# A tile per half for layer 0's state, sums moved within steps, and outer products spread over other steps, in a two-layer recurrent kernel

## The chip, the cores and the metric

The kernel runs on one core of a Trainium2 chip. The metric is device time in microseconds (us) for one execution. The kernel before takes 1827.79 us (median of 3 runs, 1827.32 to 1827.85). Beside the timed runs there is one profiled execution, and every duration quoted below is from it.

## What is computed

Two recurrent layers over 128 sequences of 128 steps with 512 features, each with a residual, all in float32:

```python
def layer0(x, h, W, b, alpha):          # W is 512 x 1024
    Wh, Wz, leak = W[:, :512], W[:, 512:], 1.0 - alpha
    def step(h, z_t):
        gate = sigmoid(h @ Wh.T + z_t @ Wz.T + b)
        h = tanh(h * leak + gate * z_t)
        return h, h
    ...
def layer1(x, h, Wx, Wh, b):
    xw = x @ Wx + b                      # for all steps
    def step(h, xw_t):
        h = tanh(xw_t + h @ Wh)
        return h, h
    ...
x = x + layer0(x, cond, ...)
x = x + layer1(x, cond, ...)
```

The products with `Wh` have to go step by step. The products of the inputs (`z_t @ Wz.T` and `x @ Wx`) do not depend on the recurrence.

## The kernel before

**Layout.** Features lie on the 128 partitions: a state of one step is a tile of 128 partitions by 4 blocks of 128 features by 128 sequences (`[P, C, P]`, C = 4). "Half 0" of a state is feature blocks 0 and 1, "half 1" blocks 2 and 3. Weights are the stationary operand.

**Steps and groups.** Time runs over steps t = 0 to 136. Layer 0 works on its time t in step t, layer 1 on its time u = t - 9 (`LAG`). Four steps make a group (`G = 4`); k is the place of a step in its group, g the group's number. A step's work on TensorE is, in this order: layer 0's state product (`L0.state_product`, both halves, 3.57 us), layer 1's state product (3.57 us), and some of the *outer products* that prepare the inputs of a later group.

**Input products by Strassen's scheme.** The input product of a whole group is done with seven products in place of eight, numbered 1 to 7 and run in the order `OUTER = 1, 5, 6, 3, 7, 2, 4`. For layer 1 this is one level (`Layer.multiply`: eight matmul instructions of 256 columns, 1.73 us). For layer 0 it is two levels (`DeepLayer.multiply_deep`: each outer product is again seven inner products, in the order `INNER = 1, 2, 6, 3, 7, 4, 5`, 1.56 us), but for its group 1, which is one level, and its group 0, whose inputs are multiplied directly in steps (`input_product`).

The products need sums of activations. Sums of the outer level are made by GpSimd (`add_up`, tiles `sa` for layer 0 and `sb` for layer 1; numbers 5, 6, 3 and 7). Sums of the inner level for layer 0 are made by VectorE (`add_up_inner`, tile `inner`): with `kind` 0 from the activations themselves, called *raw* here, with `kind` 1 from GpSimd's outer sums, called *nested*. A nested sum reads all four of GpSimd's sums. Outer product 1 reads raw sums, outer product 5 nested ones.

Results of products go through PSUM banks A0, A1, B0 and B1. For layer 1, products 1, 6, 7 and 4 share bank B0, products 5 and 3 share B1, product 2 has A1. After each product its bank is read: products 1, 5 and 6 are copied by ScalarE into kept tiles, 3, 7 and 2 are added to a kept tile by VectorE (`add`, L283; `add_deep`, L418), and 4 is copied out last. Product 4 adds onto what stands in the bank of product 7, so it may start only when the add of product 7 has read that bank. For layer 0's deep products, `gather` (VectorE) then combines the parts.

**A step of layer 0.** Before its state product, the bank of the step is filled with the input part: `seed_deep` on VectorE (on ScalarE for group 1). The bank tile `ra` spans two PSUM banks, one per half; it has one buffer, so `bank_of(t + 1)` waits until step t's bank has been read. The state product adds onto it. Then for each half i: `gate0` (ScalarE, two sigmoids), `mix0` (VectorE, one multiplication and two multiply-adds), `tanh0` (ScalarE), and `residual` (GpSimd, adds the state to the activation in place). The next step's state product needs both halves of the new state.

**A step of layer 1.** It has a tile for each half, `r0b` and `r1b`: `seed` (ScalarE) fills it, the state product adds onto it, `tanh1` reads it, `residual` adds it to the activation, and `finish` transposes the result on VectorE to `o` (L168) and stores it.

**Inputs.** `load_x` brings the input of step t + 8 by DMA from SyncE, `prepare_x` transposes it on VectorE (L163) into the group's tile `T`.

**Order of the work.** Each engine works its instructions strictly in the order given. That order is written out by hand: `at(time, fn, ...)` puts a piece of work into a plan with a due time, and at the end the pieces are issued in the order of their due times. A due time sets the order and nothing else; an engine starts an instruction as soon as those before it are done and its inputs are there. `start[t]` is the planned start of step t, worked out from the planned durations (`STATE`, `PRODUCT`, `DEEP`) and from `shares(t)`, which says for each step which outer products of which layer and group it does:

- k = 0: layer 1, group g - 2, products 7, 2, 4
- k = 1: layer 0, group g + 1, products 1, 5, 6, 3
- k = 2: layer 0, group g + 1, products 7, 2, 4
- k = 3: layer 1, group g - 1, products 1, 5, 6, 3

Before step 0, group 1's products 1, 5, 6, 3 and 7 of layer 0 are done; products 2 and 4 follow in steps 3 and 4. In the step with k = 0 that starts at `a` (the next one starting at `b`), GpSimd's sums for group g + 1 are due at a+0.8, 0.9, 4.8 and 8.4; VectorE's raw sums 5, 6, 3 and 7 at a+6.0, 6.7, 7.4 and 9.6, its nested ones at a+11.4, a+12.0, b+5.9 and b+6.6. Layer 0's mix of half 0 is due at a+2.29, of half 1 at a+4.07, the seed of the next step at a+5.31, the adds of layer 1's products 7 and 2 at a+8.92 and a+10.65.

Of the kernel before, what the change touches and what calls it, by code (L numbers as in the profile page):

```python
# [7 lines left out]
F32 = mybir.dt.float32  # L8
AF = mybir.ActivationFunctionType
ALU = mybir.AluOpType  # L10
# [3 lines left out]
def kernel(  # L14
# [56 lines left out]
    psum = ctx.enter_context(tc.tile_pool(name="psum", bufs=1, space=bass.MemoryType.PSUM))  # L71
# [3 lines left out]
    def at(time, fn, *args):  # L75
        plan.append((time, len(plan), fn, args))


    STATE, PRODUCT, DEEP = 3.57, 1.73, 1.56
    OUTER = 1, 5, 6, 3, 7, 2, 4  # L80

    def shares(t):

        g, k = divmod(t, G)
        if t < 5:
            return {3: [(0, 1, OUTER[5:6])], 4: [(0, 1, OUTER[6:])]}.get(t, [])
        said = (
            [(1, g - 2, OUTER[4:])], [(0, g + 1, OUTER[:4])],
            [(0, g + 1, OUTER[4:])], [(1, g - 1, OUTER[:4])],
        )[k]  # L90
        return [x for x in said if 0 <= x[1] < NG]

    start, clock = [], 24.3
# [44 lines left out]
    per_feature = const.tile([P, 3, C], F32, tag="per_feature", name="per_feature")  # L138
# [77 lines left out]
    class Layer:  # L216
# [104 lines left out]
        def state_product(self, t, half, h):  # L321
            alone = (t, half) not in self.state
            ps = self.state_bank(t, half) if alone else self.state[t, half]
            for m in range(2):
                for c in range(C):
                    nc.tensor.matmul(  # L326
                        ps[:, m], self.wh[:, c, 2 * half + m, :], h[t - 1][:, c],
                        start=alone and m == 0 and c == 0, stop=c == C - 1, skip_group_check=True,
                    )
# [3 lines left out]
    class DeepLayer(Layer):  # L333
# [118 lines left out]
            eng.tensor_tensor(c[:, :, 2:4], c[:, :, 2:4], c[:, :, 0:7:6], ALU.add)  # L452
            eng.tensor_tensor(c[:, :, 4], c[:, :, 4], c[:, :, 2], ALU.add)

        def bank_of(self, t):
            self.state[t] = psum.tile([P, 2, 4, P], F32, tag="ra", name=f"ra_{t}")
            return self.state[t][:, :, 0:2]

        def seed_deep(self, t):
            g, k = divmod(t, G)  # L460
            c = self.parts[g, k // H]
            out = self.bank_of(t)
            if g == 1:
                nc.scalar.copy(out, c[:, :, k % H : 4 : H])  # L464
            elif k % H == 0:
                nc.vector.tensor_tensor(out, c[:, :, 0:3:2], c[:, :, 1:4:2], ALU.add)  # L466
            else:
                u3 = c[:, :, 4:5].broadcast_to([P, 2, 2, P])
                nc.vector.tensor_tensor(out, c[:, :, 5:7], u3, ALU.add)  # L469

        def state_product(self, t, half, h):
            for m in range(2):
                for c in range(C):
                    nc.tensor.matmul(  # L474
                        self.state[t][:, half, m], self.wh[:, c, 2 * half + m, :], h[t - 1][:, c],
                        start=False, stop=c == C - 1, skip_group_check=True,
                    )

        def input_product(self, t):

            g, k = divmod(t, G)
            ps = self.bank_of(t)
            for c in range(C):
                for m in range(C):
                    nc.tensor.matmul(
                        ps[:, m // 2, m % 2], self.w[:, c, m, :], ring[g][:, c, k],
                        start=c == 0 and m % 2 == 0, stop=False, skip_group_check=True,
                    )

    L0, L1 = DeepLayer("a"), Layer("b")  # L490
    ring = {}
    h0, h1, s0 = {-1: condT}, {-1: condT}, {}
# [14 lines left out]
    def gate0(t, i):  # L507
        if i == 0:
            s0[t] = work.tile([P, C, P], F32, tag="s", name=f"s_{t}")
            h0[t] = hpool.tile([P, C, P], F32, tag="h0", name=f"h0_{t}")  # L510
        for m in range(2):
            f = 2 * i + m
            nc.scalar.activation(  # L513
                s0[t][:, f], L0.state[t][:, i, m], AF.Sigmoid, bias=per_feature[:, 0, f : f + 1]
            )

    def mix0(t, i):
# [48 lines left out]
    for i, time in ((5, 16.2), (6, 17.4), (3, 18.7), (7, 20.0)):  # L566
        at(time, L0.add_up, 1, i)
    L0.products(1, OUTER[:1], 14.4)
    L0.products(1, OUTER[1:5], 17.4)
    at(18.2, from_natural, condT, cond_in)  # L570
    for kc in range(C):
        at(18.9 + 0.6 * kc, transpose_w0, L0.wh, "wh0", kc)
# [15 lines left out]
    for t in range(T + LAG):  # L588
        g, k = divmod(t, G)
        now = start[t]  # L590
        if AHEAD <= t + AHEAD < T:
            at(now + 0.01, load_x, t + AHEAD)
        if t < T:
            for i in range(2):
                end = now + STATE * (1 + i) / 2
                at(now + STATE * i / 2, L0.state_product, t, i, h0)
                at(end + 0.05, gate0, t, i)
                at(end + 0.5, mix0, t, i)
                at(end + 1.75, tanh0, t, i)
                at(end + 2.3, residual, t, i, h0)  # L600
            if G <= t + 1 < T:
                at(start[G] - 0.9 if t == G - 1 else end + 1.74, L0.seed_deep, t + 1)
            now += STATE
        if t < G - 1:
            at(now + 0.6, L0.input_product, t + 1)
            now += STATE
        u = t - LAG
        if u >= 0:
            for i in range(2):
                end = now + STATE * (1 + i) / 2  # L610
                at(now + STATE * i / 2, L1.state_product, u, i, h1)
                at(end + 0.05, tanh1, u, i)
                if u + 1 < T:
                    at(end + 0.5 if (u + 1) % G else now + STATE + 2 * PRODUCT + 0.1, L1.seed, u + 1, i)
                at(end + 0.6, residual, u, i, h1)
            at(start[t + 1] + 0.6 if u + 1 < T else end + 1.4, finish, u)
            now += STATE
        for layer, group, which in shares(t):
            if layer == 1:
                now = L1.products(group, which, now)  # L620
            elif group == 1:
                now = L0.products(group, which, now)
            else:
# [56 lines left out]
```

## Time and profile before

| what | us |
|---|---|
| median of 3 runs | 1827.79 |
| profiled execution, its own time | 1823.2 |
| its span, first to last instruction | 1821.4 |
| TensorE busy in it | 1694.3 (93%), 13108 matmul instructions |
| VectorE busy | 1047.6 (58%), 1804 instructions |
| ScalarE busy | 657.4 (36%), 1792 instructions |
| GpSimd busy | 806.9 (44%), 788 instructions |
| mean granted TensorE clock | 0.990 |

In the names of the profile PE is TensorE, PEld its weight loads, DVE VectorE, ACT ScalarE, POOL GpSimd and SP SyncE; L474 is line 474 of the kernel. A line of a group or a timeline names the engine, the line, the operation, and output <- input. `ra` is layer 0's state bank, `B_b` one of the product banks B0 and B1 used by layer 1. A float32 matmul of 128 by 128 stands in it as two instructions, so that a state product has 32.

Some step starts of the profiled execution, read from the first matmul of layer 0's state product (layer 1's in step 128):

| step | starts at (us) |
|---|---|
| 0 | 28.3 |
| 3 | 59.0 |
| 4 | 68.8 |
| 6 | 97.2 |
| 8 | 120.8 |
| 12 | 176.55 |
| 40 | 564.2 |
| 41 | 579.1 |
| 42 | 593.2 |
| 43 | 605.0 |
| 44 | 619.1 |
| 124 | 1721.4 |
| 128 | 1764.8 |
| end of the span | 1821.4 |

The four steps from 564.2 are a group in the middle of the run, and those on either side of it look the same. VectorE is busy there for 10.6, 8.6, 8.0 and 6.2 us of the four steps, GpSimd for 10.0, 7.4, 4.1 and 3.5 us, and the 16 DMA engines for about a fifth of the time.

### The profile page before, as it was taken

The page shows a single profiled execution, that of the slowest core. Times are in us where ns is not written, and L with a number is a line of the kernel's source. Part 1 is how long each engine was busy: PE and PEld are TensorE (multiplying, and loading weights), DVE is VectorE, ACT ScalarE, POOL GpSimd, SP SyncE. Part 2 cuts the span into 40 slices and gives each one's busy share as a digit, 9 for nine tenths or more (in the row PEclk, how much of TensorE's full clock was granted, in tenths as well). Part 3 has the DMA queues.
Part 4 walks back from the last instruction along what each step waited for, and adds up shares of the span by engine and source line. Part 5 has one row for each costly group of instructions (what it writes and reads, how often), then busy time and mean ns, then how long its engine had stood idle before and what let it go on. Part 6 is the DMA issues. An engine that isn't in the chain of part 4 may idle for free.

```text
span 1821.4 us, 33397 instructions
## 1 busy us (share of the span) xinstructions
PE 1694.3 (93%) x13108; PEld 1623.3 (89%) x13108; DVE 1047.6 (58%) x1804; ACT 657.4 (36%) x1792; POOL 806.9 (44%) x788
## 2 busy tenths in 40 slices
PE   5789999999999999999999999999999999999998
PEld 5679988899988998988999989899889999889988
DVE  4455666655656656656556656556666556566431
ACT  1233333333333344333333333333333333333433
POOL 3443454443445444444434444434544444454343
PEclk9899999999999999999999999999999999999999
DMA  8101111111211121111121111111111112111112
GB/s 168 36 7 31 40 36 36 42 41 36 45 38 36 36 47 36 40 43 36 36 47 36 36 41 42 36 44 39 36 35 42 41 36 47 36 36 24 25 29 48
DMA packets 153213, 73.78 MB, mean 41 GB/s; under 512 B 16800, under 2 KB 151968, under 8 KB 153056
## 3 DMA queue, kind: packets, MB, share of 16 engines
q1 hardware_dynamic: 148992, 69.53, 17.2%
q10 hardware_dynamic: 3840, 1.84, 0.5%
q8 instruction: 104, 1.70, 0.4%
q14 instruction: 53, 0.43, 0.1%
q0 software_dynamic: 224, 0.27, 0.1%
HBM read 38.02 MB, written 33.55 MB: 39 GB/s over the span
## 4 chain that ended last, share of the span: by engine, by line
PE 71%; DVE 21%; ACT 6%; issue 1%; DMA 1%; POOL 0%; ACTq 0%; POOLq 0%; DVEq 0%
PE ra L474 25%; PE B_b L257 16%; PE A_a L392 8%; DVE inner L199 7%; PE r0b L326 7%; PE r1b L326 7%; PE B_a L392 7%; DVE s L521 6%; ACT s L513 4%; DVE s L519 4%; ACT h L526 2%; DVE cb L283 1%; DVE ra L469 1%; DVE ra L466 1%; DMA x<-in_x_dram 1%
## 5 line engine op out<-in xcount | busy, mean ns | idle before, releaser
L530 POOL TENSOR_TENSOR T<-T,h 128x256 f32<-128x256 f32 x512 | 454.9, 902 | 838.3 <-ACT h L526 800.7
L474 PE MATMUL ra<-h,wha 128*128 128x128 f32 x4064 | 486.0, 279 | 11.1 <-ACT ra L464 6.4
L474 PEld LDWEIGHTS ra<-h,wha 128*128 128x128 f32 x4064 | 480.3, 196 | 16.1 <-ACT ra L464 7.2
L519 DVE TENSOR_TENSOR s<-s,T 128x256 f32<-128x256 f32 x256 | 133.5, 522 | 419.1 <-ACT s L513 419.1
L513 ACT ACTIVATE s<-ra,per_feature 128x128 f32<-128x128 f32 x512 | 158.3, 360 | 492.1 <-PE ra L474 484.8
L326 PE MATMUL r0b<-h,whb 128*128 128x128 f32 x2032 | 249.0, 275 | 0.1
L326 PE MATMUL r1b<-h,whb 128*128 128x128 f32 x2032 | 247.7, 275 | 0.0
L326 PEld LDWEIGHTS r0b<-h,whb 128*128 128x128 f32 x2032 | 237.8, 192 | 1.3 <-ACT h L541 1.1
L326 PEld LDWEIGHTS r1b<-h,whb 128*128 128x128 f32 x2032 | 237.1, 192 | 0.0
L526 ACT ACTIVATE h<-s 128x256 f32<-128x256 f32 x256 | 106.7, 417 | 352.4 <-DVE s L521 352.4
L521 DVE SCALAR_TENSOR_TENSOR s<-h,leak,s 128x128 f32<-128x128 f32 x508 | 184.0, 403 | 9.0
L257 PE MATMUL B_b<-sb,wcb 128*128 128x256 f32 x768 | 176.5, 379 | 1.9 <-ACT kb_p L266 1.9
L199 POOL TENSOR_TENSOR sa<-T 128x512 f32<-128x512 f32 x62 | 94.4, 1522 | 167.5 <-DVE T L163 167.5
L257 PEld LDWEIGHTS B_b<-sb,wcb 128*128 128x128 f32 x768 | 141.3, 190 | 22.5 <-issue 2.3
L392 PE MATMUL A_a<-inner,wia 128*128 128x128 f32 x720 | 139.9, 276 | 0.0
L257 PE MATMUL B_b<-T,wcb 128*128 128x256 f32 x256 | 66.5, 404 | 68.9 <-DVE cb L283 68.9
L257 PEld LDWEIGHTS B_b<-T,wcb 128*128 128x128 f32 x256 | 47.4, 194 | 86.0 <-DVE cb L283 80.5
L392 PE MATMUL B_a<-inner,wia 128*128 128x128 f32 x540 | 107.6, 281 | 11.2 <-DVE inner L199 11.1
L392 PEld LDWEIGHTS A_a<-inner,wia 128*128 128x128 f32 x720 | 110.0, 193 | 0.0
L283 DVE TENSOR_TENSOR cb<-B_b,kb_u 128x512 f32<-128x512 f32 x32 | 22.1, 692 | 149.5 <-PE B_b L257 149.5
L168 DVE STREAM_TRANSPOSE o<-T 128x512 f32<-128x512 f32 x128 | 90.0, 703 | 28.4 <-POOL T L530 25.2
L418 DVE TENSOR_TENSOR ca<-B_a,ka_u 128x512 f32<-128x512 f32 (+1 forms) x60 | 36.9, 625 | 107.6 <-PE B_a L392 107.6
(124 smaller groups left out, 2339.7 us busy)
## 6 DMA issues: line engine op xcount, KB each, us to landing
out_dram<-o SPq DMA_DIRECT2D x510, 64.0 KB, 1.8
x<-in_x_dram SPq DMA_DIRECT2D x502, 64.0 KB, 2.5
wx_in<-in_L_cond_Wx_dram SPq DMA_DIRECT2D x4, 256.0 KB, 5.8
wh_in<-in_L_cond_Wh_dram SPq DMA_DIRECT2D x4, 256.0 KB, 7.5
x<-in_x_dram ACTq DMA_DIRECT2D x10, 64.0 KB, 3.9
wz_in<-in_L_cond_W_dram ACTq DMA_DIRECT2D x2, 256.0 KB, 6.5
wz_in<-in_L_cond_W_dram SPq DMA_DIRECT2D x2, 256.0 KB, 6.0
wh_in<-in_L_cond_W_dram ACTq DMA_DIRECT2D x2, 256.0 KB, 6.4
```

Source lines behind the costliest of these rows:

```text
L168: nc.vector.transpose(dst.rearrange("p a (c j) -> p c a j", j=S), src.rearrange("p c (a i) -> p c a i", i=S))
L199: eng.tensor_tensor(out(SUM[which]), one(), two(), op)
L257: nc.tensor.matmul(ps[:, m], w[:, c, m, :], a[:, c], start=first and m == 0 and c == 0, stop=c == 1, skip_group_check=True,)
L283: nc.vector.tensor_tensor(self.result(g, i, half), banks[tag], self.kept[kept], ALU.add)
L326: nc.tensor.matmul(ps[:, m], self.wh[:, c, 2 * half + m, :], h[t - 1][:, c], start=alone and m == 0 and c == 0, stop=c == C - 1, skip_grou ...
L392: nc.tensor.matmul(banks[f"{tag}{part}"][:, place], self.right_inner(outer, i), self.left_inner(g, outer, i), start=first and place == 0, ...
L474: nc.tensor.matmul(self.state[t][:, half, m], self.wh[:, c, 2 * half + m, :], h[t - 1][:, c], start=False, stop=c == C - 1, skip_group_che ...
L513: nc.scalar.activation(s0[t][:, f], L0.state[t][:, i, m], AF.Sigmoid, bias=per_feature[:, 0, f : f + 1])
L519: nc.vector.tensor_tensor(s[:, two[i]], s[:, two[i]], at_of(t)[:, two[i]], ALU.mult)
L521: nc.vector.scalar_tensor_tensor(s[:, m], h0[t - 1][:, m], leak[:, m : m + 1], s[:, m], ALU.mult, ALU.add)
L526: nc.scalar.activation(h0[t][:, two[i]], s0[t][:, two[i]], AF.Tanh)
L530: nc.gpsimd.tensor_tensor(r, r, h[t][:, two[i]], ALU.add)
```

## The change

The state bank of layer 0 loses its own tile over two banks; layer 0 now uses the same `state_bank` and `state_product` as layer 1, with tiles `r0a` and `r1a`, one per half. `seed_deep` takes a half and makes one instruction per half, due behind the mix of its half. `gate0` takes its half's tile.

```diff
-        def bank_of(self, t):
-            self.state[t] = psum.tile([P, 2, 4, P], F32, tag="ra", name=f"ra_{t}")
-            return self.state[t][:, :, 0:2]
-
-        def seed_deep(self, t):
+        def seed_deep(self, t, half):
             g, k = divmod(t, G)
-            c = self.parts[g, k // H]
-            out = self.bank_of(t)
+            c = self.parts[g, k // H][:, half]
+            out = self.state_bank(t, half)
             if g == 1:
-                nc.scalar.copy(out, c[:, :, k % H : 4 : H])
+                nc.scalar.copy(out, c[:, k % H : 4 : H])
             elif k % H == 0:
-                nc.vector.tensor_tensor(out, c[:, :, 0:3:2], c[:, :, 1:4:2], ALU.add)
+                nc.vector.tensor_tensor(out, c[:, 0:3:2], c[:, 1:4:2], ALU.add)
             else:
-                u3 = c[:, :, 4:5].broadcast_to([P, 2, 2, P])
-                nc.vector.tensor_tensor(out, c[:, :, 5:7], u3, ALU.add)
-
-        def state_product(self, t, half, h):
...
+                nc.vector.tensor_tensor(out, c[:, 5:7], c[:, 4:5].broadcast_to([P, 2, P]), ALU.add)
...
-            ps = self.bank_of(t)
+            ps = [self.state_bank(t, half) for half in range(2)]
...
-                        ps[:, m // 2, m % 2], self.w[:, c, m, :], ring[g][:, c, k],
+                        ps[m // 2][:, m % 2], self.w[:, c, m, :], ring[g][:, c, k],
...
+        ps = L0.state.pop((t, i))
         for m in range(2):
             f = 2 * i + m
             nc.scalar.activation(
-                s0[t][:, f], L0.state[t][:, i, m], AF.Sigmoid, bias=per_feature[:, 0, f : f + 1]
+                s0[t][:, f], ps[:, m], AF.Sigmoid, bias=per_feature[:, 0, f : f + 1]
             )
...
-            if G <= t + 1 < T:
-                at(start[G] - 0.9 if t == G - 1 else end + 1.74, L0.seed_deep, t + 1)
+                if G <= t + 1 < T:
+                    at(end + 1.66, L0.seed_deep, t + 1, i)
```

The sums of activations get other due times within the step with k = 0 and the one behind it, with their own times for the first such step (t = 4), where they are due in step 3 and at the start of step 4:

```diff
-            a, b, f = start[t], start[t + 1], 0.5 if t == G else 1.0
+            a, b = start[t], start[t + 1]
             if g + 1 < NG:
-                for i, time in ((5, 0.8), (6, 0.9), (3, 4.8), (7, 8.4)):
-                    at(a + f * time, L0.add_up, g + 1, i)
-                for i, time in ((5, 6.0), (6, 6.7), (3, 7.4), (7, 9.6)):
-                    at(a + f * time, L0.add_up_inner, g + 1, 0, i, nc.vector)
-                for i, time in ((5, a + 11.4 * f), (6, a + 12.0 * f), (3, b + 5.9 * f), (7, b + 6.6 * f)):
-                    at(time, L0.add_up_inner, g + 1, 1, i, nc.vector)
+                for i, pool, raw, nested in (
+                    (5, a + 1.5, a + 1.45, b + 1.45), (6, a + 7.0, a + 5.8, b + 5.8),
+                    (3, a + 9.0, a + 6.5, b + 6.5), (7, a + 10.0, a + 7.2, b + 7.2),
+                ):
+                    if t == G:
+                        n = (5, 6, 3, 7).index(i)
+                        pool, raw, nested = start[3] + 2.5 + n, start[3] + 5.8 + 0.1 * n, a + 0.2 + 0.1 * n
+                    at(pool, L0.add_up, g + 1, i)
+                    at(raw, L0.add_up_inner, g + 1, 0, i, nc.vector)
+                    at(nested, L0.add_up_inner, g + 1, 1, i, nc.vector)
...
-            at((start[2] + 1.1, start[3] + 0.5, start[3] + 1.2, start[3] + 4.5)[t], prepare_x, t + AHEAD)
+            at((start[2] + 1.1, start[2] + 6.0, start[3] + 0.3, start[3] + 1.0)[t], prepare_x, t + AHEAD)
```

The outermost products of the first and last groups go to other steps. At the start: group 1's product 2 before step 0 (its product 4 in step 3), group 2's products 1 and 5 in step 4, 6 and 3 in step 5. At the end: group 30's products of layer 1 in steps 125 to 127, group 31's in steps 128 to 132, where they stood in 127 and 128, and in 131 and 132. The planned start of step 0 goes from 24.3 to 26.0, and the seed of layer 1 at a group's border may be due earlier:

```diff
-        if t < 5:
-            return {3: [(0, 1, OUTER[5:6])], 4: [(0, 1, OUTER[6:])]}.get(t, [])
-        said = (
-            [(1, g - 2, OUTER[4:])], [(0, g + 1, OUTER[:4])],
-            [(0, g + 1, OUTER[4:])], [(1, g - 1, OUTER[:4])],
-        )[k]
+        if t <= G + 1:
+            return {
+                3: [(0, 1, OUTER[6:])], 4: [(0, 2, OUTER[:2])], 5: [(0, 2, OUTER[2:4])]
+            }.get(t, [])
+        if g == NG - 1:
+            said = (
+                [(1, g - 2, OUTER[4:])], [(1, g - 1, OUTER[:2])],
+                [(1, g - 1, OUTER[2:4])], [(1, g - 1, OUTER[4:])],
+            )[k]
+        elif t >= T:
+            said = [(1, NG - 1, (OUTER[0:1], OUTER[1:2], OUTER[2:3], OUTER[3:5], OUTER[5:])[t - T])] if t < T + 5 else []
+        else:
+            said = (
+                [(1, g - 2, OUTER[4:])], [(0, g + 1, OUTER[:4])],
+                [(0, g + 1, OUTER[4:])], [(1, g - 1, OUTER[:4])],
+            )[k]
...
-    L0.products(1, OUTER[1:5], 17.4)
+    L0.products(1, OUTER[1:6], 17.4)
...
-                    at(end + 0.5 if (u + 1) % G else now + STATE + 2 * PRODUCT + 0.1, L1.seed, u + 1, i)
+                    due = min(now + STATE + 2 * PRODUCT + 0.1, start[t + 1] - 0.05)
+                    at(end + 0.5 if (u + 1) % G else due, L1.seed, u + 1, i)
```

More of the change, by code (lines that the diff above doesn't have):

```diff
@@ L84, in shares @@
         g, k = divmod(t, G)
-        if t < 5:
-            return {3: [(0, 1, OUTER[5:6])], 4: [(0, 1, OUTER[6:])]}.get(t, [])
-        said = (
-            [(1, g - 2, OUTER[4:])], [(0, g + 1, OUTER[:4])],
-            [(0, g + 1, OUTER[4:])], [(1, g - 1, OUTER[:4])],
-        )[k]
+        if t <= G + 1:
[14 more added lines that the diff above has]
+            )[k]
         return [x for x in said if 0 <= x[1] < NG]
-    start, clock = [], 24.3
+    start, clock = [], 26.0
     for t in range(T + LAG + 4):
@@ L453, in gather @@
             eng.tensor_tensor(c[:, :, 4], c[:, :, 4], c[:, :, 2], ALU.add)
-        def bank_of(self, t):
-            self.state[t] = psum.tile([P, 2, 4, P], F32, tag="ra", name=f"ra_{t}")
-            return self.state[t][:, :, 0:2]
-        def seed_deep(self, t):
+        def seed_deep(self, t, half):
             g, k = divmod(t, G)
-            c = self.parts[g, k // H]
-            out = self.bank_of(t)
+            c = self.parts[g, k // H][:, half]
+            out = self.state_bank(t, half)
             if g == 1:
-                nc.scalar.copy(out, c[:, :, k % H : 4 : H])
+                nc.scalar.copy(out, c[:, k % H : 4 : H])
             elif k % H == 0:
-                nc.vector.tensor_tensor(out, c[:, :, 0:3:2], c[:, :, 1:4:2], ALU.add)
+                nc.vector.tensor_tensor(out, c[:, 0:3:2], c[:, 1:4:2], ALU.add)
             else:
-                u3 = c[:, :, 4:5].broadcast_to([P, 2, 2, P])
-                nc.vector.tensor_tensor(out, c[:, :, 5:7], u3, ALU.add)
-        def state_product(self, t, half, h):
[L472 to L477, printed above, removed]
+                nc.vector.tensor_tensor(out, c[:, 5:7], c[:, 4:5].broadcast_to([P, 2, P]), ALU.add)
         def input_product(self, t):
             g, k = divmod(t, G)
-            ps = self.bank_of(t)
+            ps = [self.state_bank(t, half) for half in range(2)]
             for c in range(C):
```

## The prediction

> **What bounds the kernel now.** I read the page's busy shares first, then the waits of each engine, then the timelines of TensorE, VectorE, ScalarE and GpSimd through one group of four steps in the middle of the run, and through the first 180 us and the last 100.
>
> TensorE is busy for 1694.3 of 1821.4 us, so what can be had is mostly its idle time. The waits say whom it waits for (total us, times, longest):
>
> ```profile
> ACT s L513 <- PE ra L474: 484.8, 126, 5.9
> PE B_b L257 <- DVE cb L283: 68.9, 29, 2.8
> PE B_a L392 <- DVE inner L199: 12.9, 30, 1.0
> ```
>
> The second line comes once a group of four steps, always at one place. The timeline of TensorE in the step that starts at 564.21 (start, duration, engine, line, operation):
>
> ```profile
> 564.21 3.73 PE L474 MATMUL ra<-h,wha 128*128 128x128 f32 x32
> 573.08 1.89 PE L257 MATMUL A_b<-T,wb 128*128 128x256 f32 x8
> 577.31 1.99 PE L257 MATMUL B_b<-T,wcb 128*128 128x256 f32 x8 [2.34 <-DVE cb L283]
> ```
>
> Product 7 of layer 1 ends at 573.08, product 2 at 574.81, and product 4, which writes the bank of product 7 again, starts only at 577.31: 2.50 us lost. VectorE shows why:
>
> ```profile
> 571.69 1.50 DVE L521 SCALAR_TENSOR_TENSOR s<-h,leak,s 128x128 f32<-128x128 f32 x2
> 573.11 0.69 DVE L469 TENSOR_TENSOR ra<-ca 128x512 f32<-128x512 f32 x1
> 573.72 0.68 DVE L199 TENSOR_TENSOR inner<-T 128x512 f32<-128x512 f32 x1
> 574.43 1.10 DVE L199 TENSOR_TENSOR inner<-inner,T 128x512 f32<-128x512 f32 x1
> 575.56 1.09 DVE L199 TENSOR_TENSOR inner<-T,inner 128x512 f32<-128x512 f32 x1
> 576.58 0.68 DVE L283 TENSOR_TENSOR cb<-B_b,kb_p 128x512 f32<-128x512 f32 x1
> ```
>
> The add that frees the bank (L283) could run at 573.1 and stands behind the second mix of layer 0, the seed and three raw sums. The mix is late because its gate is late: the gate of half 0 starts behind the whole state product, though its own half ended 1.79 us earlier. Layer 1 has a tile per half; near the end, its tanh of half 0 starts 0.26 us into half 1's product:
>
> ```profile
> 567.98 0.63 ACT L513 ACTIVATE s<-ra,per_feature 128x128 f32<-128x128 f32 x2 [4.46 <-PE ra L474]
> 1779.22 1.95 PE L326 MATMUL r1b<-h,whb 128*128 128x128 f32 x16
> 1779.48 0.38 ACT L541 ACTIVATE h<-r0b 128x256 f32<-128x256 f32 x1 [1.34 <-PE r0b L326]
> ```
>
> The first steps have no layer 1 beside them, and there the chain gate, mix, tanh itself sets the step:
>
> ```profile
> 62.62 1.89 PE L257 MATMUL B_a<-T,wa 128*128 128x256 f32 x8
> 68.78 6.53 PE L474 MATMUL ra<-h,wha 128*128 128x128 f32 x32 [4.27 <-ACT ra L464]
> ```
>
> Beside the idle 4.27 us the state product took 6.53 where it takes 3.73 elsewhere; the granted clock is 0.83 from 60 to 100 us.
>
> **The tile per half.** No matmul is added or removed. The seed of a step becomes two instructions: on VectorE 120 of 0.69 us become 240 of about 0.41 (the 128x256 adds of L539), 0.13 us a step more, and on ScalarE four copies become eight. They run while VectorE waits for the gates (1.06 to 2.4 us a time); without that cover it is 16 us over the run. What it moves is the chain. With S the start of the state product: gate 0 at S+1.79+0.26=2.05 (before 3.77); mix 0 at 2.71 (0.66 after the gate, as in the rows); tanh 0 at 3.88 (1.17 later); gate 1, behind it on ScalarE, at 4.20; mix 1 at 4.88; tanh 1 at 6.08; the next state product can start at 6.80 (0.72 later, from 1741.39 to 1742.11). The same rows gave 8.5 before, which is what steps 125 and 126 measure (8.51 and 8.58).
>
> **A steady group.** Step 4g, with a its start and 12.33 us of products (two states of 3.57, three products of 1.73). Before mix 0 VectorE was idle for 2.26 us; raw sum 5 (0.68) goes there. GpSimd's sum 5 starts at 2.31 as before and now meets raw sum 5 and mix 0. Three residuals took 3.52 us against raw sums, 2.19 alone, and a mix whose first instruction met a GpSimd sum took 0.77, not 0.42. So mix 1 ends between 6.0 and 7.4. Behind it stand seed 1 (0.35 apart), raw 6, 3 and 7 (1.13, 1.02, 0.60), then the add: it starts between 9.1 and 10.5, and 0.72 later product 4 may go, wanted at 10.60. The wait is 0 to 0.6; I take 0.2.
>
> [...]
>
> GpSimd's sums 6, 3 and 7 are moved behind two, three and three more residuals. Counting from 2.31: sum 5 to about 4; the residuals when their tanh is done (5.6, 8.2, 9.4); sum 6 to 10.9; the last residual 11.6; sum 3 12.9; sum 7 14.2, that is b+1.9 with b the next start. Behind these stand layer 1's sum 5 (wanted a step later) and the next residuals, which wait for tanh until b+4.3 anyway. VectorE's transposes to o and of x come first; then nested sum 5 waits for sum 7, with mix 0 of the next step queued behind it. It ends near b+3.2, mix 0 moves from b+2.7 to b+3.2, and nested 7 ends at about b+9.2. The product that reads it wants it at b+9.59 (product 5 starts at 8.70, its fifth matmul 0.89 later). Before, it came 0.54 too late; now the wait is 0 to 0.4, I take 0.1. If sum 7 came 1 us later, that cover would be gone.
>
> Steps 4g+2 and 4g+3 lost nothing (11.84 and 14.06) and gain nothing. So the group falls from 54.87 to 51.65 plus 0.3. The mean from 176.55 to 1721.44 (28 groups) is 55.18, since five groups took some 1.7 us more, with slower products behind the wait; that goes too. 28 x (55.18-51.95) = **-90**. Bounds of the added waits: 0 to 1.0 a group, 99 to 70.
>
> **The start.** Product 2 of group 1 before step 0: +1.73. Steps 0 to 2 measured 10.2: the input product waits for the bank until gate 1 is done (2.8 us idle). With two tiles its first four matmuls go at once, the rest at S+4.86, ending at 8.0: 3 x 2.2 = 6.6 less. Step 3: 9.7 to 6.8 (product 4 is inside the chain). Step 4: all eight raw and nested sums now stand ahead of its mix on VectorE: 3.45+2.9 us from S3+5.95, mix 0 at S3+12.3, the next state at S3+16.4, so 9.6 against 13.0. Step 5 has two products instead of four: 6.9 against 15.4. Steps 6 and 7: 8.8 and 10.6 against 11.0 and 12.6, the waits of 2.48 (L418) and 1.89 (kept copy) nearly gone, since their engines reach them 1.7 us earlier. Steps 8 to 11: 51.0 against 55.7. Step 12 starts at 147.8, not 176.5. TensorE idles 3.3 us before step 5; between 2.91 (no slowing) and 4.27 (2.8 us lost) I charge half of 2.8. So **-27**, bounds -18 to -32. The x transposes that go with it (tiles 9 to 11 earlier, and with them the freed load slots) find their data: the last wait for x is over by 18 us.
>
> [...]
>
> **The end.** Group 30's and 31's products fill steps 125 to 131. That removes the idle 1.20 twice in steps 125 and 126 and 0.3 twice or three times in the lone steps: **-3.3**, bounds -1 to -4.
>
> **Sum.** 1821.4-90-27-3.3 = 1701. The median of the runs stands 6.4 above the span of the profiled one (1827.8; its own time was 1823.2), so **1707**.
>
> **Rivals.** (1) *The add stays late* (0.12): GpSimd's sum wins the start of each mix, and product 4 still waits 1.5 us. For: the 0.77 and 1.50 us mixes. Against: VectorE's back-to-back sums ran unslowed. A group is 53.2, 28 x (55.18-53.2) = 55: 1821.4-55-27-3+6.4 = **1743**.
> (2) *The split does not start the gate earlier* (0.08), the change not doing what it says: then mix 1 still ends at 8.9 and the add comes at about 12.4 as before, nested 7 some 0.6 later with nested 6 in front of it: +17 in 28 groups, the start -15 (step 5 and half of step 4), the end -3, about **1827**. Against it: layer 1's tanh.
> (3) *Slower: nested 5 blocks VectorE* (0.05). It waits for GpSimd's sum 7 ahead of the next mix. From b+2.3 on, each us that sum 7 is late reaches product 5. The gains are used up when TensorE loses 4.3 us a group (120/28), with sum 7 at b+6.6, if GpSimd's eight instructions took half as long again. At 5 us lost: 1707+28x5 = **1847**. For: eight instructions in one queue; against: the sum above has 4.7 us to spare.
>
> **How the numbers follow.** The forecast has 0.75; its own range is 1693 to 1739 (the bounds of the group's waits, the start and the end together). With (1) and a little beyond it the range to hold 8 in 10 is 1692 to 1747. The measurement tells 0.2% from no change. Faster: forecast, (1) and part of (2), 0.90; same 0.04, slower 0.06, from (2) and (3).
>
> **What would show it.** Right: gate 0 about 2.05 after the state's start; the wait of B_b for cb below 0.5 us a time; steady groups near 52 us; steps 3 to 7 together near 43 us (before 61.8). Wrong: L199 inner on VectorE waiting long for GpSimd's sa, or mix 0 starting past b+4; the add still ending past a+10.6; a granted clock below 1 past step 12.

## The result and the profile after

The kernel after the change takes 1735.25 us (median of 4 runs, 1735.09 to 1736.9), the kernel before on the same chip 1827.82 us (4 runs, 1827.32 to 1829.13): a ratio of 0.9495, interval 0.9478 to 0.9511. That is 92.6 us less, where 120.8 were forecast; it lies inside the range.

The page of the profile after (span, then busy time, share of the span and number of instructions of each engine):

```profile
span 1733.5 us, 33461 instructions
PE 1683.9 (97%) x13108; PEld 1617.3 (93%) x13108; DVE 1061.2 (61%) x1924; ACT 667.3 (38%) x1796; POOL 788.4 (45%) x788
```

TensorE's share went from 93% to 97%: with the same 13108 matmul instructions, what is gone is mostly idle time (127.1 us before, 49.6 after). Busy time fell by 10.4 us, so the same instructions also ran a little faster on average. The waits of the kernel after (total us, times, longest) answer to those shown before:

```profile
ACT s L511 <- PE r0a L336: 254.5, 127, 5.1
DVE inner L209 <- POOL sa L209: 30.6, 29, 1.8
PE B_a L402 <- DVE inner L209: 11.1, 31, 1.2
PE B_b L267 <- DVE cb L293: 8.8, 29, 0.4
```

The gates wait half as long for the state (254.5 against 484.8 us). TensorE's wait for the add that frees layer 1's bank fell from 68.9 to 8.8 us. It did not go quite to nothing, its wait for nested sums hardly changed (before 12.9), and VectorE's wait for GpSimd's sums doubled (before 15.8).

To compare stages, the span is cut at the first matmul of layer 0's state product of each step. The places k = 0 to 3 of a step in its group are medians over the 28 groups from step 12 to step 124; the column "group" is the mean length of these 28 groups (us):

| kernel | median of runs | ratio to before | span | step 12 starts | group | k = 0 | k = 1 | k = 2 | k = 3 | step 124 to end |
|---|---|---|---|---|---|---|---|---|---|---|
| before | 1827.8 | | 1821.4 | 176.4 | 55.17 | 14.95 | 14.04 | 11.84 | 14.06 | 100.1 |
| after | 1735.3 | 0.9495 | 1733.5 | 160.2 | 52.74 | 12.89 | 13.95 | 11.84 | 14.06 | 96.7 |
| e1_split_only | 1758.7 | 0.9696 | 1755.3 | 159.4 | 53.52 | 14.23 | 13.40 | 11.84 | 14.06 | 97.4 |
| e2_no_split | 1808.4 | 0.9971 | 1809.8 | 179.0 | 54.79 | 13.71 | 15.18 | 11.84 | 14.06 | 96.7 |
| e3_old_sums | 1754.7 | 0.9675 | 1752.5 | 157.4 | 53.52 | 14.23 | 13.40 | 11.84 | 14.06 | 96.7 |
| e4_mix_first | 1711.6 | 0.9438 | 1710.1 | 159.6 | 51.92 | 12.33 | 13.70 | 11.84 | 14.06 | 96.7 |
| c1_after | 1735.9 | 0.9491 | 1733.6 | 160.1 | 52.74 | 12.89 | 13.95 | 11.84 | 14.06 | 96.7 |
| e5_late_sum | 1715.9 | 0.9382 | 1713.9 | 156.1 | 52.18 | 12.89 | 13.40 | 11.84 | 14.06 | 96.7 |
| e6_both | 1700.0 | 0.9295 | 1698.3 | 156.3 | 51.62 | 12.33 | 13.40 | 11.84 | 14.06 | 96.7 |
| e7_start | 1698.8 | 0.9288 | 1696.3 | 154.3 | 51.62 | 12.33 | 13.40 | 11.84 | 14.06 | 96.7 |

E1 to E4 were run together on one chip, against 13 runs of the kernel before with a median of 1814.69 (1805.79 to 1821.83); C1 and E5 to E7 together on another chip, against 7 runs with a median of 1828.64 (1825.04 to 1832.97). The kernel before is 0.8% faster on the first of these chips, so runs of the two chips are compared by the stages and by C1, and not by the ratio: E4's 1711.6 is faster than E5's 1715.9 although its ratio is larger.

The account of the span, before to after: the start 176.4 to 160.2, **-16.2**; 28 groups from 55.17 to 52.74, **-68.2**; the end 100.15 to 96.68, **-3.5**. Together -87.9 of 1821.4. (The 176.55 and 1721.44 that stand ahead of this section for steps 12 and 124 are the ends of the matmul before; the steps start at 176.39 and 1721.27. The mean group is the same by either.)

The timeline of TensorE in the kernel after, in the middle of the run (start, duration, engine, line, operation):

```profile
529.37 1.95 PE L336 MATMUL r0a<-h,wha 128*128 128x128 f32 x16
...
538.24 1.89 PE L267 MATMUL A_b<-T,wb 128*128 128x256 f32 x8
540.43 1.99 PE L267 MATMUL B_b<-T,wcb 128*128 128x256 f32 x8 [0.30 <-DVE cb L293]
542.26 1.95 PE L336 MATMUL r0a<-h,wha 128*128 128x128 f32 x16
...
552.31 0.49 PE L402 MATMUL B_a<-inner,wia 128*128 128x128 f32 x2 [0.29 <-DVE inner L209]
```

and ScalarE's first gate of that step:

```profile
531.35 0.63 ACT L511 ACTIVATE s<-r0a,per_feature 128x128 f32<-128x128 f32 x2 [2.67 <-PE r0a L336]
```

The gate comes 1.98 us after the start of the state product (before 3.77). Product 4 starts 2.19 us behind product 2, whose length is 1.73: 0.46 lost, and 0.10 more since its first matmuls are slower behind a wait (1.99 for 1.89); before it was 2.50. The second wait is that of outer product 5 for nested sum 7, in the next step.

VectorE in the same two steps:

```profile
531.58 0.69 DVE L209 TENSOR_TENSOR inner<-T 128x512 f32<-128x512 f32 x1
532.18 1.49 DVE L517 TENSOR_TENSOR s<-s,T 128x256 f32<-128x256 f32 x1
533.71 0.62 DVE L519 SCALAR_TENSOR_TENSOR s<-h,leak,s 128x128 f32<-128x128 f32 x2
...
539.69 0.68 DVE L293 TENSOR_TENSOR cb<-B_b,kb_p 128x512 f32<-128x512 f32 x1
...
544.08 1.74 DVE L209 TENSOR_TENSOR inner<-sa 128x512 f32<-128x512 f32 x1 [1.00 <-POOL sa L209]
545.75 0.41 DVE L517 TENSOR_TENSOR s<-s,T 128x256 f32<-128x256 f32 x1
...
551.05 1.21 DVE L209 TENSOR_TENSOR inner<-sa 128x512 f32<-128x512 f32 x1
```

and GpSimd beside it:

```profile
531.68 1.71 POOL L209 TENSOR_TENSOR sa<-T 128x512 f32<-128x512 f32 x1 [7.33 <-DVE T L173]
...
542.77 1.27 POOL L209 TENSOR_TENSOR sa<-T 128x512 f32<-128x512 f32 x1
544.00 1.28 POOL L209 TENSOR_TENSOR sb<-T 128x512 f32<-128x512 f32 x1
```

The first multiplication of a mix takes 0.41 alone (545.75) and 1.49 at 532.18. GpSimd's sum 5 was issued at 531.68, 0.10 behind raw sum 5 on VectorE; it took 1.71 where it takes 1.27 alone, and ended at 533.39, and the mix's multiplication ended at 533.67. So the three ended one after the other: raw 5 at 532.27, then GpSimd's sum, then the mix's multiplication. In the next step nested sum 5 (544.08) meets layer 1's sum 5 on GpSimd (544.00) and takes 1.74 for 0.69. These two meetings are what the experiments were aimed at.

The second meeting was there before the change too. VectorE's nested sum 5 and GpSimd's sum 5 of layer 1 in the kernel before:

```profile
579.02 1.74 DVE L199 TENSOR_TENSOR inner<-sa 128x512 f32<-128x512 f32 x1 [0.57 <-POOL sa L199]
578.95 1.27 POOL L199 TENSOR_TENSOR sb<-T 128x512 f32<-128x512 f32 x1
```

There, too, nested 5 took 1.74, so its price could have been read in that profile.

### The profile page after: what moved, and what is told of

The parts are those of the page before. It is cut to its first block, busy times and chain, and to the rows that moved or that the text cites. A ratio compares the mean times of both kernels' runs of the same rounds, so it can differ in the third digit from the quotient of the medians.

```text
span 1733.5 us, 33461 instructions
## 1 busy us (share of the span) xinstructions
PE 1683.9 (97%) x13108; PEld 1617.3 (93%) x13108; DVE 1061.2 (61%) x1924; ACT 667.3 (38%) x1796; POOL 788.4 (45%) x788
## 4 chain that ended last, share of the span: by engine, by line
PE 58%; DVE 22%; POOL 12%; ACT 5%; issue 2%; DMA 1%; DVEq 0%; SPq 0%; ACTq 0%; POOLq 0%
PE B_b L267 13%; DVE inner L209 9%; PE A_a L402 8%; PE r0b L336 7%; PE r1b L336 7%; POOL sa L209 7%; PE r0a L336 7%; PE B_a L402 7%; PE r1a L336 7%; DVE s L517 5%; DVE s L519 5%; POOL T L528 5%; ACT h L524 2%; ACT s L511 2%; DVE o L178 1%
## 5 line engine op out<-in xcount | busy, mean ns | idle before, releaser
L528 POOL TENSOR_TENSOR T<-T,h 128x256 f32<-128x256 f32 x512 | 420.1, 832 | 712.4 <-ACT h L524 637.4
L517 DVE TENSOR_TENSOR s<-s,T 128x256 f32<-128x256 f32 x256 | 153.8, 601 | 170.0 <-ACT s L511 170.0
L336 PE MATMUL r0a<-h,wha 128*128 128x128 f32 x2032 | 250.1, 276 | 6.1 <-ACT h L524 6.0
L336 PEld LDWEIGHTS r0a<-h,wha 128*128 128x128 f32 x2032 | 243.7, 193 | 10.1 <-ACT h L524 6.9
L336 PE MATMUL r1a<-h,wha 128*128 128x128 f32 x2032 | 249.2, 276 | 0.0
L336 PEld LDWEIGHTS r1a<-h,wha 128*128 128x128 f32 x2032 | 238.9, 193 | 0.0
L511 ACT ACTIVATE s<-r0a,per_feature 128x128 f32<-128x128 f32 x256 | 80.2, 364 | 254.5 <-PE r0a L336 254.5
L519 DVE SCALAR_TENSOR_TENSOR s<-h,leak,s 128x128 f32<-128x128 f32 x508 | 164.8, 366 | 9.0
L402 PE MATMUL B_a<-inner,wia 128*128 128x128 f32 x540 | 108.2, 282 | 10.5 <-DVE inner L209 10.5
L209 DVE TENSOR_TENSOR inner<-sa 128x512 f32<-128x512 f32 x60 | 86.2, 1436 | 30.6 <-POOL sa L209 30.6
```

Of the source, the lines that this page charges most:

```text
L209: eng.tensor_tensor(out(SUM[which]), one(), two(), op)
L336: nc.tensor.matmul(ps[:, m], self.wh[:, c, 2 * half + m, :], h[t - 1][:, c], start=alone and m == 0 and c == 0, stop=c == C - 1, skip_grou ...
L402: nc.tensor.matmul(banks[f"{tag}{part}"][:, place], self.right_inner(outer, i), self.left_inner(g, outer, i), start=first and place == 0, ...
L511: nc.scalar.activation(s0[t][:, f], ps[:, m], AF.Sigmoid, bias=per_feature[:, 0, f : f + 1])
L517: nc.vector.tensor_tensor(s[:, two[i]], s[:, two[i]], at_of(t)[:, two[i]], ALU.mult)
L519: nc.vector.scalar_tensor_tensor(s[:, m], h0[t - 1][:, m], leak[:, m : m + 1], s[:, m], ALU.mult, ALU.add)
```

## The experiments

All kernels compute the whole reference. Step numbers and places are those of the text above.

### E1: the split alone

The kernel before, with layer 0's state in a tile per half and a seed per half; the sums and the outer products stand where they stood before.

```diff
-            if G <= t + 1 < T:
-                at(start[G] - 0.9 if t == G - 1 else end + 1.74, L0.seed_deep, t + 1)
+                if G <= t + 1 < T:
+                    at(start[G] - 0.9 + 0.01 * i if t == G - 1 else end + 1.66, L0.seed_deep, t + 1, i)
```

> The kernel before with the split alone (a tile and a seed per half); sums and products stay where they were before. Theory A, that the early gate is what frees layer 1's add: the gate starts 2.05 us after the state product's start, mix 1 ends near a+6.9, the add stands behind seed and raw sums 5, 6 and 3 and ends near a+10.5, so product 4 waits under 0.3 us, and nested 7 comes in time too: a steady group near 52 us (before 55.18, after 52.74), the start some 8 us shorter, the end as before, in all about 1720 to 1730. Rival B, that the moved sums do the work and the split is only their condition: a group of 54 us or more, 1790 to 1820.

Measured: 1758.72 us, ratio 0.9696 (0.9667 to 0.9724). The group is 53.52, so a steady group near 52 from the split alone was wrong, and so was rival B's 54 or more. Step 12 starts at 159.4, as early as in the kernel after: 17.0 earlier than before, where some 8 were expected. VectorE in a step with k = 0 of E1 (the gate is L501 here, the mix L507 and L509):

```profile
536.71 1.23 DVE L507 TENSOR_TENSOR s<-s,T 128x256 f32<-128x256 f32 x1 [0.47 <-ACT s L501]
537.97 1.50 DVE L509 SCALAR_TENSOR_TENSOR s<-h,leak,s 128x128 f32<-128x128 f32 x2
...
541.10 1.50 DVE L509 SCALAR_TENSOR_TENSOR s<-h,leak,s 128x128 f32<-128x128 f32 x2
...
545.72 0.68 DVE L283 TENSOR_TENSOR cb<-B_b,kb_p 128x512 f32<-128x512 f32 x1
```

GpSimd in the same step:

```profile
536.38 1.27 POOL L199 TENSOR_TENSOR sa<-T 128x512 f32<-128x512 f32 x1 [7.33 <-DVE T L163]
537.73 1.33 POOL L199 TENSOR_TENSOR sa<-sa,T 128x512 f32<-128x512 f32 x1
...
540.74 1.45 POOL L199 TENSOR_TENSOR sa<-T,sa 128x512 f32<-128x512 f32 x1
```

and the waits of E1:

```profile
PE B_b L257 <- DVE cb L283: 47.4, 29, 1.7
```

The mixes come early, and each meets a GpSimd sum: 1.23 for 0.42, and twice 1.50 for 0.62. This is what rival (1) of the prediction describes, "GpSimd's sum wins the start of each mix", here with the sums at their old places: the wait at product 4 is 1.63, where the rival had 1.5, and the group 53.52, where it had 53.2. The nested wait is gone (k = 1 falls to 13.40).

### E2: all but the split

The kernel after, with before's single tile over two banks and its one seed.

```diff
-        def seed_deep(self, t, half):
+        def bank_of(self, t):
+            self.state[t] = psum.tile([P, 2, 4, P], F32, tag="ra", name=f"ra_{t}")
+            return self.state[t][:, :, 0:2]
+
+        def seed_deep(self, t):
...
-                if G <= t + 1 < T:
-                    at(end + 1.66, L0.seed_deep, t + 1, i)
+            if G <= t + 1 < T:
+                at(start[G] - 0.9 if t == G - 1 else end + 1.74, L0.seed_deep, t + 1)
```

> The changed kernel with the old bank tile over two banks and one seed a step; moved sums and spread products stay. Theory A: mix 1 still ends near a+8.9, the add ends near a+12.5 as before, nested 6 stands in front of 3 and 7, a steady group of 54.9 to 55.5; the end 3.3 us shorter, the start some 5 to 12 shorter: 1805 to 1825. Rival B: a group of 53.5 or less, 1760 to 1780.

Measured: 1808.43 us, ratio 0.9971 (0.9953 to 0.9989): next to nothing. The waits of E2:

```profile
PE B_a L402 <- DVE inner L209: 37.7, 59, 1.1
PE B_b L267 <- DVE cb L293: 33.1, 29, 1.9
```

The wait for the add is halved (before 68.9), and that for the nested sums has tripled (before 12.9): k = 0 wins 1.24 and k = 1 loses 1.14. Step 12 starts at 179.0, 2.6 later than before, where a start 5 to 12 shorter was expected. So the moved sums and the spread products are worth almost nothing without the split; the end, at 96.7, is the one part that gains as much without it.

### E3: the split and the spread products, with the old sums

The kernel after, with before's due times of the sums in steady groups. The first group's sums stay where the change put them.

```diff
-                    (5, a + 1.5, a + 1.45, b + 1.45), (6, a + 7.0, a + 5.8, b + 5.8),
-                    (3, a + 9.0, a + 6.5, b + 6.5), (7, a + 10.0, a + 7.2, b + 7.2),
+                    (5, a + 0.8, a + 6.0, a + 11.4), (6, a + 0.9, a + 6.7, a + 12.0),
+                    (3, a + 4.8, a + 7.4, b + 5.9), (7, a + 8.4, a + 9.6, b + 6.6),
```

> The changed kernel with the sums of the steady groups at the due times of before (the first group's sums, the split and the spread products stay). Theory A: groups as in the split alone, near 52, so 10 to 25 us faster than the changed kernel, 1710 to 1725. Rival B: the moves of the sums are worth something, a group above 53, 1745 or more.

Measured: 1754.70 us, ratio 0.9675 (0.9641 to 0.9709). The group is E1's, 53.52: the spread does nothing in steady groups. Groups near 52 and 1710 to 1725 us were wrong again; rival B, that the moves of the sums are worth something, holds. Step 12 starts at 157.4, 2.8 earlier than after. Of this 1.8 lies in steps 8 to 11 (53.5 for 55.2), where the new places of the sums cost time: the nested sums come too late. The other 1.1 are there before step 8, up to which the two kernels do the same work in the same order: the second half of step 6's state product took 1.95 there, and 3.21 in the kernel after.

The steady group, split by parts: from 54.88 (the typical group before) the split alone takes 1.36, the sums alone 0.09, both 2.14. The remaining 0.69 are there only with both.

### E4: the mix ahead of raw sum 5

The kernel after. Raw sum 5 goes behind the mix of half 0, and in steps with k = 0 the transpose of x stands ahead of that to `o`, so that GpSimd's sum 5, which waits for it, starts earlier.

```diff
-            at(start[t + 1] + 0.7, prepare_x, t + AHEAD)
+            at(start[t + 1] + (0.5 if k == G - 1 else 0.7), prepare_x, t + AHEAD)
...
-                    (5, a + 1.5, a + 1.45, b + 1.45), (6, a + 7.0, a + 5.8, b + 5.8),
+                    (5, a + 1.5, a + 2.4, b + 1.45), (6, a + 7.0, a + 5.8, b + 5.8),
```

> The changed kernel with raw sum 5 behind mix 0, and in the step with k = 0 the transpose of x in front of that to o. Theory C, that what is left of layer 1's wait is the mix of half 0 held up by GpSimd's sum 5, which gets in while raw sum 5 runs (the multiplication takes 1.49 us there, alone 0.42): the multiplication takes under 0.8 us, the add ends about 0.5 to 1 us earlier, product 4 waits for nothing, a group near 52.2, so 12 to 16 us faster than the changed kernel, 1719 to 1723. Rival D, that VectorE has simply too much to do ahead of the add, whatever the order: the add ends at the same place, 1733 to 1737.

Measured: 1711.64 us, ratio 0.9438 (0.9410 to 0.9466); the group 51.92, k = 0 at 12.33. VectorE in a step of E4 that starts at 523.10:

```profile
525.74 0.63 DVE L517 TENSOR_TENSOR s<-s,T 128x256 f32<-128x256 f32 x1 [0.47 <-ACT s L511]
...
526.94 0.68 DVE L209 TENSOR_TENSOR inner<-T 128x512 f32<-128x512 f32 x1
...
532.61 0.68 DVE L293 TENSOR_TENSOR cb<-B_b,kb_p 128x512 f32<-128x512 f32 x1
```

GpSimd and TensorE beside it:

```profile
524.83 1.27 POOL L209 TENSOR_TENSOR sa<-T 128x512 f32<-128x512 f32 x1 [6.74 <-DVE T L173]
```

```profile
531.98 1.89 PE L267 MATMUL A_b<-T,wb 128*128 128x256 f32 x8
533.70 1.89 PE L267 MATMUL B_b<-T,wcb 128*128 128x256 f32 x8
```

GpSimd's sum now takes its 1.27, beside a transpose and VectorE's wait for the gate, and is over at 526.10; the mix's multiplication, begun 0.36 before that, takes 0.63 instead of 1.49. The add starts 9.51 us into the step (10.32 in the kernel after), and product 4 follows product 2 with no gap. No work was taken away, and the same four raw sums still stand ahead of the add; only the order changed, so rival D is out. This confirms the meeting with GpSimd's sum 5 as the cause of the wait. The gain is larger than expected: 0.82 a group, where a group near 52.2 would have been 0.5. The edit moved both pieces together; what each is worth by itself was not tried. The step behind it gains 0.25 as well (13.70 for 13.95).

### C1: the kernel after again

The kernel after unchanged, as a yardstick on the second chip.

> The changed kernel once more, as the yardstick for the runs beside it: a steady group of 52.74 us, 5% below the kernel before on the same chip.

Measured: 1735.92 us, ratio 0.9491 (0.9472 to 0.9511); all stages within 0.1 us of those of the kernel after.

### E5: layer 1's sums 5 and 6 later

The kernel after. GpSimd does layer 1's sums 5 and 6 in the last quarter of the step with k = 1, not at its start.

```diff
-                    at(one + (0.04, 0.55)[n % 2] * (after - one), L1.add_up, g - 1, i)
+                    at(one + ((0.75, 0.8) if n < 2 and g < NG - 1 else (0.04, 0.55))[n % 2] * (after - one), L1.add_up, g - 1, i)
```

> The changed kernel with layer 1's sums 5 and 6 on GpSimd moved to the last quarter of the step with k = 1. Theory C (VectorE's sums lose their time to GpSimd sums running at the same moment): nested sum 5 takes 0.7 us instead of 1.74, mix 0 of that step starts by b+2.9 instead of b+3.5, nested 7 ends before product 5 wants it; the step with k = 1 falls from 13.96 to 13.4, a group 52.2, 15 us less than the changed kernel. Rival D (nested 7 is late by GpSimd's sum 7 alone, which nested 5 waits for): k = 1 stays at 13.8 or more, no difference above 4 us.

Measured: 1715.91 us, ratio 0.9382 (0.9360 to 0.9405); the group 52.18, k = 1 at 13.40. VectorE in the step of E5 that starts at 534.28, and the waits of E5:

```profile
536.10 0.69 DVE L209 TENSOR_TENSOR inner<-sa 128x512 f32<-128x512 f32 x1 [1.00 <-POOL sa L209]
...
542.24 1.21 DVE L209 TENSOR_TENSOR inner<-sa 128x512 f32<-128x512 f32 x1
```

```profile
PE B_a L402 <- DVE inner L209: 1.1, 2, 0.6
PE B_b L267 <- DVE cb L293: 8.8, 29, 0.4
```

Nested sum 5 takes 0.69 for 1.74, and TensorE's wait for nested sums is gone from all steady groups, with VectorE's wait for GpSimd's sum 7 unchanged at 1.00. So it was not the waiting for sum 7 that made nested 7 late, but what ran beside nested 5. The other wait stays at 8.8, as it should. Step 12 starts 4.0 earlier than in C1, which was not expected and makes the whole 20 us less than C1, not 15.

### E6: both

E4's and E5's edits together.

> Raw sum 5 behind mix 0 and x ahead of o (as in e4_mix_first) together with the late sums of layer 1 (as in e5_late_sum). Theory C: both waits of the group gone, 51.65 a group, TensorE's own work, so 28 x 1.1 = 31 us less than the changed kernel. Rival D: as e4_mix_first, 51.9, 23 us less.

Measured: 1700.01 us, ratio 0.9295 (0.9276 to 0.9315). The waits of E6:

```profile
PE B_a L402 <- DVE inner L209: 1.1, 2, 0.6
PE B_b L267 <- DVE cb L293: 0.5, 1, 0.5
```

The group is 51.62, 1.12 less than in the kernel after: 0.57 in k = 0 and 0.56 in k = 1, both waits and nothing else. 12.33 is the length of the products of a step with k = 0 (two states of 3.57, three products of 1.73). The groups give 28 x 1.12 = 31.4 of the 35.3 us by which the span is shorter than C1's, the start the other 3.9.

### E7: work moved out of step 5

E6, with the permutations of layer 1's state weights on ScalarE and the combinations of its input weights on GpSimd due in step 6.

```diff
-        at(start[4] + 5.0 + 0.5 * kc, permute_w1, L1.wh, "wh1", kc)
+        at(start[6] + 5.5 + 0.5 * kc, permute_w1, L1.wh, "wh1", kc)
...
-        at(start[5] + 1.3 * n, L1.combine_weights, i, nc.gpsimd)
+        at(start[6] + 4.5 + 1.3 * n, L1.combine_weights, i, nc.gpsimd)
```

> As e6_both, and at the start layer 1's state weights are permuted by ScalarE in step 6 instead of 4, and its weight combinations made by GpSimd from the middle of step 6 instead of step 5. Theory E, that step 5 (10.0 us against the 6.9 forecast) is long because its gate stands behind three permutes on ScalarE and its mixes run beside GpSimd's weight combinations: step 5 falls to 7.5 or less, step 12 starts 2 to 4 us earlier. Rival F, that the clock throttled in that stretch sets it: no difference above 1 us.

Measured: 1698.82 us, ratio 0.9288 (0.9270 to 0.9307). Step 12 starts at 154.3, 2.0 earlier than in E6, at the lower end of what was expected; the runs themselves do not tell the two kernels apart (0.07%). The gate of step 5 no longer stands behind the permutations: it comes 1.64 us after the second piece of its state product, in E6 2.21 (timeline of ScalarE in E7):

```profile
75.92 0.63 ACT L511 ACTIVATE s<-r0a,per_feature 128x128 f32<-128x128 f32 x2 [0.84 <-PE r0a L336]
```

But in step 5 layer 1's sums 5 and 6 on GpSimd then met the mix instead (the multiply-adds of half 1 took 2.58), and in step 6 one of the moved combinations and another sum did (2.51). The 10.0 us of step 5 in the expectation are counted between the second pieces of the state products (74.55 to 84.58 in the kernel after). Counted so, E7's step 5 takes 8.1 (74.28 to 82.38): shorter, but not the 7.5 expected. The two moves were not tried one by one. E7 takes 37 us less than C1 beside it, and is the fastest kernel run here.

## Why the prediction was right, and where its gain was too large

**The gate.** Forecast 2.05 us after the state's start; measured 1.98. Rival (2), that the split does not do this, is out. E1 and E2 show that it is the condition for nearly all of the gain. No run shows whether the chip or the way the program tracks its tiles made the gate of half 0 wait for half 1.

**The steady group: mechanism right, size off.** The forecast had 51.65 of TensorE's own work and 0.3 of added waits; E6 measures 51.62 for the first. The waits were 1.1, the 0.2 at product 4 being 0.57 and the 0.1 at nested 7 being 0.56, each with the slower matmuls behind the wait. 28 x 0.8 = 22 us: of the 90 forecast, 68 came. At 1.12 they are just above the bounds that were given, 0 to 1.0.

- *Product 4.* Mix 1 ended 7.2 us into the step (forecast 6.0 to 7.4) and the add started at 10.32 (9.1 to 10.5). The step that failed was the choice of 0.2 in 0 to 0.6: the sum held one mix multiplication of 0.77 beside a GpSimd sum, and there it took 1.49, since raw sum 5 in front of the mix let GpSimd's sum in between the two. Filling VectorE's idle 2.26 us with raw 5 was booked as free. It was not free of GpSimd. Rival (1) is the same mechanism at three times the price; E1 shows it at full size.
- *Nested 7.* GpSimd's sum 7 was done at b+1.78 (forecast 1.9), and VectorE did wait for it, 1.00 us, as forecast. Nested 5 then ended at b+3.56 for 3.2 and nested 7 at b+10.0 for 9.2. The forecast named layer 1's sum 5 as what stands behind sum 7 on GpSimd, and overlooked that it then starts at the same moment as nested 5. With it away (E5) nested 7 ended at b+9.17, and the wait was gone. Rival (3), the slower one, has the right place for the block, but VectorE waits only 1.00 us there, and in E5, with that wait unchanged, TensorE loses nothing by it.

**The start: -16.2 for -27.** Step 12 starts at 160.2 and not at 147.8 (149.2 with the 1.4 charged for a slower clock). The parts: step 0 starts 2.3 later (1.7 forecast); steps 0 to 2 take 26.1 (24); steps 3 and 4 together 16.4 (16.4); steps 5 and 6 together 21.0 (15.7); step 7 10.8 (10.6); steps 8 to 11 55.2 (51.0). So steps 3 to 7 take 48.2, where 43 was named as the sign. The failing step is that the chain gate, mix, tanh was put into each step with the durations of VectorE alone. In steps 1, 2 and 5 GpSimd combines weights and sums beside it, in step 3 it makes sums. Step 0, which has neither, took the 8.0 that were forecast; steps 1 and 2 took 9.1. The timeline of VectorE in steps 2 and 5 of the kernel after:

```profile
50.98 1.50 DVE L519 SCALAR_TENSOR_TENSOR s<-h,leak,s 128x128 f32<-128x128 f32 x2
...
78.08 2.51 DVE L519 SCALAR_TENSOR_TENSOR s<-h,leak,s 128x128 f32<-128x128 f32 x2
```

These are two multiply-adds that take 0.62 alone; in step 3 they took 2.51 as well. That steps 3 and 4 still come out as forecast is luck. Step 5 is counted from its first four matmul instructions, 1.41 us ahead of the rest of its state product; counted to that rest, steps 3 and 4 take 17.8.

A late mix makes TensorE wait, and behind some of these waits the granted clock was lower. TensorE in step 6:

```profile
84.58 2.01 PE L336 MATMUL r0a<-h,wha 128*128 128x128 f32 x12 [2.71 <-ACT h L524]
86.39 3.21 PE L336 MATMUL r1a<-h,wha 128*128 128x128 f32 x16
```

After 2.71 us of idleness behind a piece of 0.71 and another short gap, the second half took 3.21 for 1.95, and the granted clock from 86 to 95 us is 0.83. The forecast charged 1.4 us once, for step 5; here it came in steps 4 (0.86 from 60 to 72), 6 and 9 (0.55 from 128 to 134, behind three waits of 1.19, 0.64 and 1.19 us for nested sums). In steps 8 to 11 those late nested sums are the loss: these steps take 55.2 in the kernel after, 53.5 in E3 with the old sums, and 50.6 in E5 with GpSimd's order changed (51.0 forecast).

The prediction read the slower clock off the length of one idle stretch, between 2.91 and 4.27 us. In step 9 no wait is longer than 1.19 us; the three add up to 3.0 within 4 us, and behind them the granted clock is 0.55. Nor does the length of the wait decide alone: in E3 the same wait of 2.71 us in step 6 was followed by a second half of 1.95, in the kernel after by one of 3.21. The profile before had a case in pieces too: in its step 5, waits of 2.18 and 2.23 us with a piece of 0.71 between them, and behind them 28 matmul instructions in 6.21 us, against 3.73 for 32 elsewhere. The prediction did not use it. No run shows what sets the clock.

**The spread of the outer products.** At the start it was counted in with the split. Beside the split, E3 starts step 12 2.0 earlier than E1 (157.4 against 159.4). E3 also has the first group's sums moved, so no run gives the spread's own share. Without the split nothing is gained there (E2). At the end -3.5 for -3.3, and either the spread (E2: 96.7) or the split (E1: 97.4) gives most of that: they remove the same idle time.

**The median against the span.** It was put 6.4 above the span; it is 1.8 above. That is 4.6 us in favour, and it is luck: the prediction carried the 6.4 over from the kernel before and had no reason for it to shrink. So the span was forecast 32.5 us too short (1701 for 1733.5), 22 from the steady groups and 11 from the start, and the time 28 too short. The time is inside the range; the waits of the steady group and the start are each outside the bounds that were given for them.

## What to carry to other kernels

When an edit moves an instruction of VectorE with two inputs in SBUF into a gap, look at what GpSimd starts in that moment. Price every meeting at what is left of the other engine's instruction, and not at a share: here the meetings of one instruction with one cost 0.21 to 1.07 us, where 0.36 to 1.21 were left. The cheap remedy is order: let the GpSimd instruction run where VectorE waits for something else, as in E4, which gained 0.82 us a group. And before parts of a change are credited one by one, ask which is the condition of the others: here the moved sums alone gave 0.1 us a group, and behind the split 0.8.

## What the runs showed of the hardware

In the five meetings of one instruction of VectorE with two inputs in SBUF and one of GpSimd that follow, the one that started second took longer, not by a fixed share of its own time but by 0.13 to 0.15 us less than what was left of the other. A mix multiplication of half 0 took 0.42 us alone, 1.49 with 1.21 left of a GpSimd sum (at 532.18), 1.23 with 0.94 left (E1, at 536.71) and 0.63 with 0.36 left (E4, at 525.74); nested sum 5 took 0.69 alone (E5) and 1.74 with 1.20 left (at 544.08); a GpSimd sum took 1.27 alone and 1.71 with 0.59 left of VectorE's raw sum (at 531.68). A pair of multiply-adds took 0.62, 1.50 when it met one GpSimd instruction and 2.51 when it met two. The add of layer 1, which has one input in a product bank, was not longer in such a meeting: at 539.69 it took 0.68 with a GpSimd sum running beside it from 539.18 to 540.90, and 0.69 at 529.64 with nothing beside it.

The profile before had five groups of 56.5 among those of 54.9; in the kernel after all 28 groups lie between 52.72 and 52.75. The slower products behind the 2.5 us wait went with the wait, as forecast.
